# First expert's rows in four parts of a tile, the other experts' one-hot lanes behind them, strips that take token tiles in turn, and a GELU placed ahead of the search

## The chip, the cores and the metric

The kernel runs on one core of a Trainium2 chip. Its metric is the device time of one execution in microseconds (us), the median of several runs; lower is better. The profile is of one execution and has a time of its own.

## The reference

There are 4096 tokens of 256 features, in 8 blocks of 512. Two layers follow each other, each added to its input after a layer norm. The first is linear attention with 16 heads and an MLP (256 to 1024 to 256). The second, which the change is about, is a mixture of 8 experts in which every expert chooses its own 512 tokens:

```python
scores = jax.nn.softmax(xf @ gate_w.T, axis=-1)
vals, idx = jax.lax.top_k(scores.T, k)          # k = 4096 / 8 = 512 tokens of each expert
y = xf[flat_idx].reshape(k, n, d)               # then a layer norm of each row
h = jax.nn.gelu(jnp.einsum('knd,nfd->knf', y, fc1s) + b1s, approximate=True)
out = (jnp.einsum('knf,ndf->knd', h, fc2s) + b2s) * kept_w[..., None]
xf = xf.at[flat_idx].add(out.reshape(k * n, d))
```

All of it is in float32.

## The kernel before

**Stages.** The attention layer runs block by block, and the last block ends with the gate: logits, `lm` (L883), a difference and a product `ex` (L885, L888), an Exp on ScalarE (L892), and the scores (L898). Then a search finds each expert's threshold score: 30 bisection steps of one chain each (L1337 on VectorE, L1342 on TensorE, L1349 on VectorE), followed by prefix sums that give every chosen token a slot in its expert's list (L1365 to L1404). Then the experts are worked one after the other.

**From slots to rows.** For expert e, `mark` (L1423) builds the left operand `num` from the slots of 32 token tiles in three VectorE instructions, and `lanes` (L1433) builds a one-hot tile `hot` of 128 x 128 lanes x 32 token tiles, in two halves h of 16 token tiles each. `sums_of` (L1442) multiplies them on TensorE: 32 bf16 matmuls into one PSUM tile `pi`, 8 rounds of 4 matmuls, one for each strip of 32 rows. Strip k takes token tiles 8k to 8k+7, so each round needs both halves of `hot`. `sums_out` (L1454, ScalarE) copies `pi` out, `numbers` (L1458, one fp32 matmul, two records in the trace) folds it, and `numbers_out` (L1464, VectorE) gives the list `idx`. Four indirect DMAs on GpSimd (`gather`, L1527, issued at L1469) fetch 128 rows each into `y`.

**From rows to the first layer.** `normalised` (L1537, VectorE) scales each 128 rows, `turn` (L1549) transposes them on TensorE, `turned` (L1558, ScalarE) applies the norm's weights and makes `yT`. `hidden` (L1568) is the first expert layer: for each f of 8 groups of hidden units, `phe` sums over two halves of the features (four records of the trace, since an fp32 matmul is two), and `hidden_out` (L1577) evicts it with a GELU into `hTe`. For expert 0 the 512 rows are worked in two halves of 256 columns (`HALVES`, L1517); for the other experts in one piece of 512. `weighted` (L1586) is the second layer, `pwe`, in four row groups j. `weighted_out` (L1595, ScalarE) and `with_bias` (L1602, VectorE) finish the rows `o`, which GpSimd adds into two tables in memory (`scatter`, L1479). From expert 3 on, each expert's chosen rows are also read back from the sum table (`zg`), finished and written to the output; the other rows go by blocks (`load_z` to `store`).

**What sets the order.** Everything from L1407 on is a list of tasks for a planner (L187). A task names its engine, an assumed duration, a due time, what it comes after, and a buffer it takes; the planner goes through an assumed timeline and emits the tasks engine by engine, so each engine gets a fixed order. Four PSUM buffers (`mm`) are shared by `pi`, `pn`, `phe` and `pwe`, two (`tr`) by the transposes. Experts' index work is due 15 us earlier for each expert, so that of experts 1 to 5 stands early. What is outside the planner's lists, such as the search, is put in order by the framework at build time, engine by engine.

The order of GpSimd's gathers in this kernel is: three of expert 0, three of expert 1, the fourth of expert 0, the fourth of expert 1, then experts 2 and 3.

Of the kernel before, what the change touches and what calls it, by code (L numbers as in the profile page):

```python
# [9 lines left out]
F32 = mybir.dt.float32  # L10
# [15 lines left out]
def performer_moe_kernel(  # L26
# [18 lines left out]
    nc = tc.nc  # L45
    P = 128
# [1271 lines left out]
    def low_bits():  # L1318
        lb_i = rp.tile([P, W], I32, tag="kb", name="lb_i", bufs=2)
        nc.vector.tensor_scalar(lb_i, pTf.bitcast(I32), 0x7FFF, None, ALU.bitwise_and)  # L1320
        yield
        nc.vector.tensor_copy(kl, lb_i)
        yield
        nc.vector.tensor_scalar(khs, kh, 32768.0, None, ALU.mult)
        yield

    def largest(keys, tag, beside):
# [22 lines left out]
            u = un  # L1350
        return u

    uh = largest(kh, "h", low_bits())
    hs = small.tile([P, 1], F32, tag="hs", name="hs")
    nc.vector.tensor_scalar(hs, uh, -0.5, 32768.0, ALU.add, ALU.mult)
# [53 lines left out]
    def in_mm(name, shape, label):  # L1409
        return ps_mm.tile(shape, F32, tag=f"mm{slot[name]}", name=label, bufs=1)  # L1410
# [28 lines left out]
            lane[:, :, q], ALU.is_equal,  # L1439
        )  # L1440

    def sums_of(e):  # L1442

        pi = in_mm(("I", e), [P, P], f"pi_{e}")
        for i in range(NC // 4):
            for k in range(4):
                q = 8 * k + i
                nc.tensor.matmul(
                    pi[32 * k : 32 * k + 32, :], nums[e % 2][:, q, :], hots[e][:, :, q],
                    start=(i == 0), stop=(i == NC // 4 - 1),  # L1450
                )
        pis[e] = pi

    def sums_out(e):  # L1454
        pis["s", e] = ep.tile([P, P], F32, tag="pis", name=f"pis_{e}")
# [54 lines left out]


    ys, yTs, ggs, zgs, hTs, zs, lns, rows_o = {}, {}, {}, {}, {}, {}, {}, {}
    L0 = E - 5
    EARLY = 15.0
    AHEAD = 2.0
    SPAN = 31.0
    HALVES = (range(0, NJ // 2), range(NJ // 2, NJ))  # L1517

    def landed(name, engine, weight, place, work, after, landing, **kw):

# [124 lines left out]
        nc.vector.tensor_tensor(zj[:, 0:D], zj[:, 0:D], zj[:, D:], ALU.add)  # L1645

    kept = {}
    J = range(NJ)
    for e in range(E):
        z0 = e * SPAN  # L1650
        i0 = -EARLY * e
        def task(name, engine, weight, place, *more, z0=z0, **kw):
            add(name, engine, weight, z0 + place, *more, **kw)

        task(("M", e), "DVE", 0.8, i0 - 27, lambda e=e: mark(e), [("I", e - 2)])
        for h in range(2):
            task(
                ("L", e, h), "DVE", 1.18, i0 - 26 + h, lambda e=e, h=h: lanes(e, h),
                [("M", e)] + ([("L", e, 0)] if h else []), take=None if h else "z",
            )  # L1660
        task(("I", e), "PE", 0.8, i0 - 23, lambda e=e: sums_of(e), [("L", e, 1)], take="mm", dense=0.2)
        task(
            ("Ie", e), "ACT", 0.35, i0 - 22, lambda e=e: sums_out(e), [("I", e), ("IN", e - 2)],
            back=("I", e),
        )
        task(("IN", e), "PE", 0.3, i0 - 21, lambda e=e: numbers(e), [("Ie", e)], take="mm", dense=0)
        task(
# [3 lines left out]
        for j in J:  # L1671
            landed(
                ("G", e, j), "POOL", 1.4, -24 + 2 * j,
                lambda e=e, j=j: gather(e, j),
                [("IX", e), ("K", e - 2)]
                + [("T", e - 2, c, i) for c in range(KD) for i in range(2 if e == 2 else 1)]
                + ([("Gi", e, j - 1)] if j else []), 2.2,
            )
        halves = HALVES if e == 0 else (J,)
        for i, js in enumerate(halves):  # L1680
            task(
                ("Y", e, i), "DVE", 0.36 * len(js), -12, lambda e=e, js=js: normalised(e, js),
                [("G", e, j) for j in js],
            )
            for c in range(KD):
                task(
                    ("T", e, c, i), "PE", 0.11 * len(js), -5 + c,
                    lambda e=e, c=c, js=js, i=i: turn(e, c, js, i),
                    [("Y", e, i)], take="tr", dense=0.1,
                )  # L1690
                task(
                    ("Te", e, c, i), "ACT", 0.2 + 0.14 * len(js), -4 + c,
                    lambda e=e, c=c, js=js, i=i: turned(e, c, js, i),
                    [("T", e, c, i)] + [("H", e - 2, f, 0) for f in range(NF)]
                    + ([("H", 0, f, 1) for f in range(NF)] if e == 2 else []),
                    back=("T", e, c, i),
                )
        task(
# [6 lines left out]
                [("W", e - 2, j, 1) for j in J], 12.0,  # L1705
            )

        for i, js in enumerate(halves):
            cols = slice(js[0] * P, (js[-1] + 1) * P)
            part = 1.0 / len(halves)  # L1710
            for f in range(NF):
                task(
                    ("H", e, f, i), "PE", 1.76 * part, 1.75 * part * f + 7 * i,
                    lambda e=e, f=f, cols=cols, i=i: hidden(e, f, cols, i),
                    [("Te", e, c, i) for c in range(KD)] + ([("LW", e)] if e else []), take="mm",
                )
                task(
                    ("He", e, f, i), "ACT", 0.2 + 0.49 * part, 1.75 * part * f + 7 * i + 1,
                    lambda e=e, f=f, cols=cols, i=i: hidden_out(e, f, cols, i),
                    [("H", e, f, i)] + [("W", e - 2, j, 1) for j in J], back=("H", e, f, i),  # L1720
                )
        for j in J:
            for h in range(2):
                task(
                    ("W", e, j, h), "PE", 1.76, 15 + 3.6 * j + 1.8 * h,
                    lambda e=e, j=j, h=h: weighted(e, j, h),
                    [("He", e, f, i) for f in range(NF) for i in range(len(halves))]
                    + ([("W", e, j, 0)] if h else []),
                    take=None if h else "mm",
                )  # L1730
# [140 lines left out]
```

## Time and profile before

| what | value |
|---|---|
| median of 3 runs | 909.25 us (909.17, 909.25, 912.75) |
| the profiled execution's own time | 905.74 us |
| its span in the trace | 904.0 us |
| TensorE busy, share of the span | 804.4 us, 89% |
| VectorE, ScalarE, GpSimd busy | 67%, 40%, 32% |
| last block's gate to the search's start | 589.8 to 601.2 us |
| search and slots | 602.3 to 636.7 us |
| first expert's index work and gathers | 636.7 to 656.0 us |
| first expert's first layer (`phe`) | 652.14 to 668.3 us |
| second layer of expert 0 to that of expert 7 (`pwe` to `pwe`) | 669.08 to 890.2 us |

How to read it: times in the views are microseconds from the span's start. PE is TensorE, PEld its weight loads, DVE VectorE, ACT ScalarE, POOL GpSimd, SP the queue of plain DMAs. A row "x4" stands for four instructions that follow each other; its time is from the first start to the last end. PEclk is the share of TensorE's clock that was granted. Two views carry most of what follows: the chain that ended last, in order of time, and the timeline of all engines in a window.

### The profile page before, as it was taken

Reading aid. Unit: us, or ns where it says so; the run is one execution under the profiler, and the core shown is the slowest. Engines: PE = TensorE matmul, PEld = TensorE weight load, DVE = VectorE, ACT = ScalarE, POOL = GpSimd, SP = SyncE. Lnnn points to the kernel's source line nnn. Section 1 sums busy time; section 2 is a strip of 40 time slices with the busy share of each in tenths; the row PEclk is TensorE's granted clock in tenths of the full one; section 3 lists DMA queues with packets and bytes.
Section 4 is the critical chain, followed back from the end, with each engine's and each line's share of the span. In section 5 each row is a group of like instructions: output and inputs, shape, how many; then the busy total and the mean of one; then the engine's idle time right before and its main releaser. Section 6 shows DMA issues by size and latency. Waiting matters only on the chain.

```text
span 904.0 us, 14999 instructions
## 1 busy us (share of the span) xinstructions
PE 804.4 (89%) x5792; PEld 561.8 (62%) x5792; DVE 604.7 (67%) x1590; ACT 359.4 (40%) x662; POOL 287.0 (32%) x395
## 2 busy tenths in 40 slices
PE   5987999999899999899999989941699999999993
PEld 2665585685585685486586578721485765677663
DVE  5488658889857889867798866867922211987233
ACT  2372624644734553643463562310243223222330
POOL 5210002112102112102102101430454666785784
PEclk9988999999999999999999999955799999999997
DMA  7000001302200400300300300174135558998641
GB/s 247 1 2 1 1 2 41 100 3 70 72 1 1 140 3 33 108 2 1 125 18 2 117 3 1 58 237 172 37 112 91 143 106 240 306 275 250 193 99 41
DMA packets 61687, 78.15 MB, mean 86 GB/s; under 512 B 7984, under 2 KB 52016, under 8 KB 61488
## 3 DMA queue, kind: packets, MB, share of 16 engines
q1 hardware_dynamic: 51056, 58.87, 20.1%
q0 software_dynamic: 9856, 17.46, 8.8%
q8 instruction: 45, 0.74, 0.4%
q10 hardware_dynamic: 704, 0.87, 0.3%
q14 instruction: 26, 0.21, 0.1%
HBM read 44.01 MB, written 33.18 MB: 85 GB/s over the span
## 4 chain that ended last, share of the span: by engine, by line
PE 63%; DVE 25%; POOL 5%; issue 5%; ACT 1%; DMA 0%; POOLq 0%; DVEq 0%; ACTq 0%
PE pwe L1590 11%; PE phe L1572 10%; PE pm L862 9%; PE ph L816 7%; PE ptq L698 3%; PE pv L564 3%; PE pc L609 3%; DVE r L169 2%; DVE mxk L522 2%; PE pxk L503 2%; PE pq L440 2%; DVE kp L525 2%; PE pw L797 2%; DVE sh L672 2%; PE pdiv L729 1%
## 5 line engine op out<-in xcount | busy, mean ns | idle before, releaser
L816 PE MATMUL ph<-xaT,w_sb 128*128 128x512 f32 (+1 forms) x288 | 118.7, 552 | 0.5 <-DVE r L873 0.5
L1572 PE MATMUL phe<-yT,w1e 128*128 128x512 f32 (+1 forms) x288 | 112.5, 547 | 0.2 <-ACT yT L1562 0.2
L1590 PE MATMUL pwe<-w2e,hTe 128*128 128x256 f32 x512 | 112.4, 379 | 0.0
L862 PE MATMUL pm<-w_sb,hT 128*128 128x256 f32 x448 | 105.8, 382 | 0.0
L1590 PEld LDWEIGHTS pwe<-w2e,hTe 128*128 128x128 f32 x512 | 96.6, 190 | 14.0 <-issue 1.3
L862 PEld LDWEIGHTS pm<-w_sb,hT 128*128 128x128 f32 x448 | 81.8, 190 | 11.9 <-issue 1.8
L1572 PEld LDWEIGHTS phe<-yT,w1e 128*128 128x128 f32 x288 | 54.1, 190 | 51.9 <-issue 49.6
L816 PEld LDWEIGHTS ph<-xaT,w_sb 128*128 128x128 f32 x288 | 53.3, 192 | 44.5 <-issue 36.7
L821 ACT ACTIVATE hT<-ph,cols_sb 128x512 f32<-128x512 f32 (+1 forms) x72 | 46.0, 640 | 68.1 <-PE ph L816 62.5
L1581 ACT ACTIVATE hTe<-phe,cols_sb 128x512 f32<-128x512 f32 (+1 forms) x72 | 46.0, 640 | 66.0 <-PE phe L1572 65.9
L589 ACT ACTIVATE kp<-kp,nstab 128x256 f32<-128x256 f32 x128 | 54.5, 496 | 10.6 <-DVE nstab L553 10.6
L1469 POOL DMA_INDIRECT y<-xg,idx x32 | 37.4, 1168 | 64.0 <-DVE num L1426 41.7
L1605 DVE SCALAR_TENSOR_TENSOR o<-b2s_sb,gg,o 128x256 f32<-128x256 f32 x32 | 15.4, 483 | 60.2 <-ACT o L1598 57.5
L1483 POOL DMA_INDIRECT accs<-o,idx x28 | 47.4, 1694 | 10.7 <-issue 5.4
L522 DVE TENSOR_REDUCE mxk<-pxk 128x8 f32<-128x512 f32 x64 | 43.6, 681 | 10.4 <-PE pxk L503 10.4
L1598 ACT ACTIVATE o<-pwe,gg 128x256 f32<-128x256 f32 x32 | 15.2, 474 | 88.3 <-PE pwe L1590 88.3
L157 POOL TENSOR_SCALAR rs_b<-mv_b 128x4 f32<-128x4 f32 (+1 forms) x9 | 2.4, 262 | 145.8 <-DVE mv_b L154 145.8
L709 ACT ACTIVATE qpT<-ptq 128x512 f32<-128x512 f32 x64 | 36.2, 595 | 29.2 <-PE ptq L698 28.9
L679 DVE TENSOR_TENSOR qd<-pxq,sh 128x512 f32<-128x512 f32 x64 | 42.8, 687 | 4.5 <-PE ptq L698 2.3
L698 PE MATMUL ptq<-ident,qd 128*128 128x128 f32 x256 | 37.2, 280 | 8.6 <-DVE ex L885 8.1
L525 DVE TENSOR_TENSOR kp<-pxk,diag 128x512 f32<-128x512 f32 x64 | 43.5, 680 | 0.0
L672 DVE TENSOR_REDUCE sh<-pxq 128x8 f32<-128x512 f32 x64 | 40.8, 678 | 2.6 <-PE pxq L503 2.6
(239 smaller groups left out, 1530.3 us busy)
## 6 DMA issues: line engine op xcount, KB each, us to landing
w1e<-in_f SPq DMA_DIRECT2D x8, 1024.0 KB, 7.0
w2e<-in_f SPq DMA_DIRECT2D x8, 1024.0 KB, 8.2
z<-acc SPq DMA_DIRECT2D x8, 1024.0 KB, 8.1
x<-in_x_in SPq DMA_DIRECT2D x8, 512.0 KB, 5.8
accs<-x SPq DMA_DIRECT2D x8, 512.0 KB, 3.1
acc<-x SPq DMA_DIRECT2D x8, 512.0 KB, 4.5
xg<-xf SPq DMA_DIRECT2D x8, 512.0 KB, 3.8
accs<-xf SPq DMA_DIRECT2D x8, 512.0 KB, 4.5
```

Source lines behind the costliest of these rows:

```text
L522: nc.vector.tensor_reduce(head_cols(note("mxk", b, [P, NT, H])[:, t, :], c), pxs, AX.X, ALU.max)
L525: nc.vector.tensor_tensor(heads(get("kp", b)[:, t, :, :], c), pxs, head_cols(diag(b, 0, t), c) .unsqueeze(3).to_broadcast([P, 4, 2, M]), A ...
L589: nc.scalar.activation(kp[:, :, h, :], kp[:, :, h, :], AF.Exp, bias=nstab[:, h : h + 1])
L672: nc.vector.tensor_reduce(head_cols(kept["sh", b, t], i), pxs[:, :, i, :, :], AX.X, ALU.max,)
L698: nc.tensor.transpose(pt[:, i, :], get("qd", u)[:, 2 * hp : 2 * hp + 2, :].rearrange("p h m -> p (h m)"), ident,)
L816: nc.tensor.matmul(ph, w1_sb[:, c, ts(f, P)], get("xaT", b)[:, c, cols], start=(c == 0), stop=(c == KD - 1),)
L821: nc.scalar.activation(get("hT", b)[:, f, cols], ph, AF.Relu, bias=cols_sb[:, C_B1 + f : C_B1 + f + 1])
L862: nc.tensor.matmul(kept["PM", b, t, 0], get("hT", b)[:, f, ts(t, P)], w2_sb[:, f, :], start=(f == 0), stop=(f == NF - 1),)
L1483: this = nc.gpsimd.indirect_dma_start(out=table[:, :], out_offset=bass.IndirectOffsetOnAxis(ap=idxs[e][:, j : j + 1], axis=0), in_=src, in ...
L1572: nc.tensor.matmul(ph, w1e[:, c, ts(f, P)], yT[:, c, cols], start=(c == 0), stop=(c == KD - 1))
L1581: nc.scalar.activation(hTs[e][:, f, cols], kept["H", e, f, i], AF.Gelu_apprx_tanh, bias=cols_sb[:, col : col + 1],)
L1590: nc.tensor.matmul(kept["W", e, j], hTs[e][:, f, ts(j, P)], ws[e][1][:, f, :], start=(f == 0), stop=(f == NF - 1),)
```

## The change

Four edits go together.

1. After the search's helpers a new tile `idle` is written by a GELU on ScalarE from `one_c` (a column of ones), ahead of the call of the search in the text of the program.
2. A strip takes token tiles in turn: q is 4i + k and not 8k + i. For expert 0 `sums_of` is two tasks, rounds 0 to 3 (token tiles 0 to 15, the first half of `hot`) and rounds 4 to 7. For the other experts it stays one task.
3. The marks of experts 1 to 7, and so their lanes, come after the last part of expert 0's rows is normalised.
4. Expert 0's rows are worked in four parts of 128 columns and not in two of 256: normalising, transposes, `yT`, `phe` and its GELU. Due times follow from the number of parts.

```diff
+    idle = rp.tile([P, 1], F32, name="idle")
+    nc.scalar.activation(idle, one_c, AF.Gelu_apprx_tanh)
     uh = largest(kh, "h", low_bits())
...
-    def sums_of(e):
-        pi = in_mm(("I", e), [P, P], f"pi_{e}")
-        for i in range(NC // 4):
+    def sums_of(e, rounds=range(NC // 4)):
+        if rounds[0] == 0:
+            pis[e] = in_mm(("I", e) if len(rounds) == NC // 4 else ("Ia", e), [P, P], f"pi_{e}")
+        pi = pis[e]
+        for i in rounds:
             for k in range(4):
-                q = 8 * k + i
+                q = 4 * i + k
...
-    HALVES = (range(0, NJ // 2), range(NJ // 2, NJ))
+    PARTS = [range(j, j + 1) for j in J]
+    NPARTS = len(PARTS)
...
-        task(("M", e), "DVE", 0.8, i0 - 27, lambda e=e: mark(e), [("I", e - 2)])
+        task(
+            ("M", e), "DVE", 0.8, i0 - 27, lambda e=e: mark(e),
+            [("I", e - 2)] + ([("Y", 0, NPARTS - 1)] if e else []),
+        )
...
-        task(("I", e), "PE", 0.8, i0 - 23, lambda e=e: sums_of(e), [("L", e, 1)], take="mm", dense=0.2)
+        if e == 0:
+            task(
+                ("Ia", e), "PE", 0.7, -24, lambda e=e: sums_of(e, range(NC // 8)), [("L", e, 0)],
+                take="mm", dense=0.1,
+            )
+            task(
+                ("I", e), "PE", 0.7, -23, lambda e=e: sums_of(e, range(NC // 8, NC // 4)),
+                [("L", e, 1), ("Ia", e)], dense=0.1,
+            )
+        else:
+            task(
+                ("I", e), "PE", 1.2, i0 - 23, lambda e=e: sums_of(e), [("L", e, 1)], take="mm",
+                dense=0.2,
+            )
...
-        halves = HALVES if e == 0 else (J,)
-        for i, js in enumerate(halves):
+        parts = PARTS if e == 0 else (J,)
+        for i, js in enumerate(parts):
...
-            part = 1.0 / len(halves)
+            part = 1.0 / len(parts)
             for f in range(NF):
                 task(
-                    ("H", e, f, i), "PE", 1.76 * part, 1.75 * part * f + 7 * i,
+                    ("H", e, f, i), "PE", 1.76 * part, 1.75 * part * f + 14 * part * i,
```

The remaining lines of the diff carry the four parts into what waits for expert 0's first layer and transposes.

Since the planner replays its list, the order of every engine changes from here on. In the order of the changed program GpSimd gathers all four parts of expert 0, then all of expert 1, then of expert 2; those of expert 3 stand between the scatters of expert 0. On TensorE the transposes of the four parts stand between the first `phe` of part 0; the `pi` blocks of experts 1, 2 and 3 stand after `phe` f = 3 of part 1, after f = 4 of part 2, and after the last `phe` of part 3; the transposes of expert 1 stand within the last row group of expert 0's `pwe`. ScalarE's order around the new GELU is:

```
L944  TensorCopy plT<-pl
L1355 LoadActFuncSet
L1355 Activation idle<-one_c
L892  LoadActFuncSet
L892  Activation ex<-ex
L1460 TensorCopy pis<-pi
L1568 Activation yT<-pt_y (two)
L1587 LoadActFuncSet
L1587 Activation hTe<-phe
```

In the kernel before, `ex` follows `plT` with nothing between, and the one LoadActFuncSet of this stretch is the one ahead of the first `hTe`.

More of the change, by code (lines that the diff above doesn't have):

```diff
@@ L1451, in sums_of @@
                 )
-        pis[e] = pi
     def sums_out(e):
@@ L1512, in performer_moe_kernel @@
     ys, yTs, ggs, zgs, hTs, zs, lns, rows_o = {}, {}, {}, {}, {}, {}, {}, {}
+    J = range(NJ)
     L0 = E - 5
@@ L1647, in performer_moe_kernel @@
     kept = {}
-    J = range(NJ)
     for e in range(E):
@@ L1660, in performer_moe_kernel @@
             )
-        task(("I", e), "PE", 0.8, i0 - 23, lambda e=e: sums_of(e), [("L", e, 1)], take="mm", dense=0.2)
+        if e == 0:
[12 more added lines that the diff above has]
+            )
         task(
             ("Ie", e), "ACT", 0.35, i0 - 22, lambda e=e: sums_out(e), [("I", e), ("IN", e - 2)],
-            back=("I", e),
+            back=("I", e) if e else ("Ia", e),
         )
@@ L1675, in performer_moe_kernel @@
                 [("IX", e), ("K", e - 2)]
-                + [("T", e - 2, c, i) for c in range(KD) for i in range(2 if e == 2 else 1)]
+                + [("T", e - 2, c, i) for c in range(KD) for i in range(NPARTS if e == 2 else 1)]
                 + ([("Gi", e, j - 1)] if j else []), 2.2,
             )
-        halves = HALVES if e == 0 else (J,)
-        for i, js in enumerate(halves):
+        parts = PARTS if e == 0 else (J,)
+        for i, js in enumerate(parts):
             task(
@@ L1694, in performer_moe_kernel @@
                     [("T", e, c, i)] + [("H", e - 2, f, 0) for f in range(NF)]
-                    + ([("H", 0, f, 1) for f in range(NF)] if e == 2 else []),
+                    + ([("H", 0, f, i) for f in range(NF) for i in range(1, NPARTS)] if e == 2 else []),
                     back=("T", e, c, i),
@@ L1706, in performer_moe_kernel @@
             )
-        for i, js in enumerate(halves):
+        for i, js in enumerate(parts):
             cols = slice(js[0] * P, (js[-1] + 1) * P)
-            part = 1.0 / len(halves)
+            part = 1.0 / len(parts)
             for f in range(NF):
                 task(
-                    ("H", e, f, i), "PE", 1.76 * part, 1.75 * part * f + 7 * i,
+                    ("H", e, f, i), "PE", 1.76 * part, 1.75 * part * f + 14 * part * i,
                     lambda e=e, f=f, cols=cols, i=i: hidden(e, f, cols, i),
@@ L1717, in performer_moe_kernel @@
                 task(
-                    ("He", e, f, i), "ACT", 0.2 + 0.49 * part, 1.75 * part * f + 7 * i + 1,
+                    ("He", e, f, i), "ACT", 0.2 + 0.49 * part, 1.75 * part * f + 14 * part * i + 1,
                     lambda e=e, f=f, cols=cols, i=i: hidden_out(e, f, cols, i),
@@ L1726, in performer_moe_kernel @@
                     lambda e=e, j=j, h=h: weighted(e, j, h),
-                    [("He", e, f, i) for f in range(NF) for i in range(len(halves))]
+                    [("He", e, f, i) for f in range(NF) for i in range(len(parts))]
                     + ([("W", e, j, 0)] if h else []),
```

## The prediction

> **What bounds the kernel now.** I read the busy table by slices first, then the chain that ended last in order of time, then the timeline around the places where the chain leaves TensorE. The slices:
>
> ```profile
> PE   5987999999899999899999989941699999999993
> PEclk9988999999999999999999999955799999999997
> ```
>
> Each figure is a fortieth of the span, 22.6 us. TensorE is full except in three slices around 600 to 640 us, and there its granted clock is at half. The windows view says the same of what follows: from 669.1 to 890.2 us TensorE is busy 221.01 of 221.10 us. So whatever comes late before 669 is late at the end. The changed stretch lies there; the chain through it:
>
> ```profile
> 637.55 2.36 DVE hot L1437 x2
> ...
> 649.22 1.09 POOL y L1469
> ...
> 654.44 3.45 DMA y<-xg,idx
> 657.91 0.37 DVE y L1541
> 658.32 0.55 PE pt_y L1555 x3
> 658.87 9.50 PE phe L1572 x44
> ```
>
> The fourth gather of expert 0 is issued only at 654.44, behind three of expert 1, and TensorE waits for it until 658.32. The timeline has the rest:
>
> ```profile
> 638.83 0.38 PE L1448 MATMUL pi<-hot,num 128*32 128x128 bf16 x2 [3.96 <-DVE hot L1437]
> 639.97 1.90 PE L1448 MATMUL pi<-hot,num 128*32 128x128 bf16 x30 [0.75 <-DVE hot L1437]
> 642.90 0.16 DVE L1466 CAST idx<-pn 128x4 int32<-128x4 f32 x1
> 643.37 1.40 POOL L1469 DMA_INDIRECT y<-xg,idx  x1 [41.67 <-DVE num L1426]
> 645.07 1.89 POOL L1469 DMA_INDIRECT y<-xg,idx  x1 [0.30 <-issue]
> 652.14 4.61 PE L1572 MATMUL phe<-yT,w1e 128*128 128x256 f32 x20 [0.22 <-ACT yT L1562]
> 652.56 1.28 ACT L1581 ACT_TABLE_LOAD   x1
> ```
>
> Two matmuls of `pi` start at 638.83, and 30 must wait for the second half of `hot`. The gathers take 1.40 to 1.91 us while lanes are built on DVE, and 1.01 later. Between 641.9 and 651.1 TensorE is not idle: it does the `pi` blocks of experts 1 to 3. That decides this case.
>
> **Edit 1, the GELU.** In the built order it does not stand in the search but ahead of the last Exp, and the Exp gets a table load of its own. Here is the place:
>
> ```profile
> 598.97 0.27 ACT L944 COPY plT<-pl 128x128 f32<-128x128 f32 x1 [1.20 <-PE pl L937]
> 600.54 0.23 ACT L892 ACTIVATE ex<-ex 128x32 f32<-128x32 f32 x1 [1.31 <-DVE ex L888]
> ```
>
> ScalarE is free from 599.24. A load takes 1.28 (row 652.56), a small ACTIVATE about 0.2 (`ex` takes 0.23), a second load 1.28: with the gaps of 0.02 the Exp starts at 602.05 and not 600.54, 1.5 later. Scores, search and everything after hang on it, so **+1.5**. Bounds: 0, if the first load is hidden in some way I don't see, and 1.5; the gap of 1.31 already covers one of the loads. The load before the first `hTe` stays, since Exp has replaced the table; it is covered, because `phe` has three more PSUM buffers to run into.
>
> The row shows a GELU at 653.86, 0.02 after its load. The Trainium skill, "ScalarE: Activation LUTs", section "What ACT_TABLE_LOAD costs", adds a drain of about 1.38 to each 1.283, 2.66 per switch; by that the Exp would come 4.2 late and the sum below would be 2.7 higher. The trace shows no such drain, so I go by the row.
>
> **Edit 2, the strips.** A round of four matmuls takes 0.216 (30 in 1.90, the last lasting 0.39: 7 further rounds in 1.51). Now four rounds run beside the second half of `hot` and four after 639.97: `pi` ends 4 x 0.216 = 0.86 earlier, at 641.01. `idx` ends at 642.20 and not 643.06, as DVE is no longer building lanes; the first gather starts 0.31 later, at 642.51.
>
> **Edit 3, the lanes behind.** DVE is quiet during the four gathers, so I take 1.01 each and 0.30 between (rows from 660.65). Rows of expert 2 land 1.86 after a gather's end (1.80 to 1.92, by the starts of L1541). The four parts land at 645.4, 646.7, 648.0 and 649.3, where the last now comes at 657.9. If the first gather keeps its 1.40, all is 0.4 later. The wait put on the marks holds up DVE alone: behind it stand the marks and lanes of expert 1, done about 649.7 + 0.8 + 2.4 = 652.9; TensorE wants them about 655.
>
> From 645.4: normalise 0.35, transpose 0.44 at half clock (row 596.70), `yT` of 128 columns about 0.45 (256 take 0.56, 512 take 0.775): `phe` starts at **646.75 and not 652.14**, 5.4 earlier.
>
> **Edit 4, four parts, and what TensorE must now do.** A fp32 record with 128 columns has its price in this row:
>
> ```profile
> 69.67 0.97 PEld L774 LDWEIGHTS pr<-rden,spread 128*128 128x128 f32 x8 [0.17 <-issue]
> ```
>
> (0.97 - 0.19)/7 = 0.111, against 0.216 for 256 columns (4.61 less the last's 0.38, over 19, with one start-up gap). Part work is 8 x 4 x 4 = 128 records, 14.25 us, where 64 took 13.8: +0.45. From 646.75 to the first `pwe` TensorE has those 14.25, six transposes 0.65, three `pi` blocks 3 x 8 x 0.216 = 5.2, two `pn` 0.5: 20.6, so 667.35. The transposes of expert 1 (0.88) and a `pn` (0.25), which before lie ahead of `pwe`, lie behind: compared like with like 668.5 against 669.08, **-0.6**. The 5.4 and the stall of 1.5 go to the 5.2 of `pi`, which lost their cover.
>
> **The clock.** TensorE is now idle from 642.0 to 645.8. The windows view has the clock at 0.50 until 642.0 and 0.66 on average over 642.0 to 645.6, so it rose near 644.45, 5.6 after `pi` began. With the dense work now beginning at 645.8 I put the rise at 651.4. Until then a record takes twice as long (four `pl` of 128 columns in 1.06 at 597.82, the last 0.42: 0.214 each). Half of 4.65 us, less little waiting, is **+2.2**. Bounds: 0, if the clock is up at 646.75, and 4.2, if it takes as long as the row that is worst here (589.9 to 600.0: TensorE busy 7.49 of 10.10 at clock 0.50), a rise at 655.8. I take the 5.6, the same matmuls in the same place.
>
> "TensorE: Matmul & The Clock Gate", Part 1, speaks against this edit too: full clock comes after a busy window of some 3.4 us, whose start is not tied to the kernel. As an estimate by that page the rise is 3.4 to 6.8 after 645.8, and the sum +1.4 to +3.0.
>
> **The end.** The tail's order changes. Now:
>
> ```profile
> 890.15 0.47 ACT L1598 ACTIVATE o<-pwe,gg 128x256 f32<-128x256 f32 x1 [2.98 <-PE pwe L1590]
> 892.17 0.48 DVE L1605 SCALAR_TENSOR_TENSOR o<-b2s_sb,gg,o 128x256 f32<-128x256 f32 x1
> ```
>
> The last `o` waits 1.55 on DVE behind the row before it, because GpSimd came to the first row's root only at 883.52. In the new order that `o` stands before the finish of row 2 (0.41 + 0.43), which comes between it and its sum: 1.55 - 0.84 = 0.7 gained, **-0.65**. Against that, GpSimd has one more output scatter (1.3) behind the last scatter-add of expert 6; if it is late there, the end is +0.65 to +1.3 instead. The rest of the dense stage has the same instructions; its new order hides under TensorE.
>
> **Sum.** +1.5 - 0.6 + 2.2 - 0.65 = **+2.45 us**. The profiled execution took 905.74 (span 904.0 and 1.7 around it), so 908.2 there. The runs' median is 3.5 above it, so I forecast 909.25 + 2.45 = **911.7**. A difference of 0.5% (4.5 us) is about what can be told from none; this is less.
>
> **Rivals.**
> 1. *Slower by over 0.5%: the half clock lasts.* ScalarE's chain in the first part (eight `yT` between GELUs, and a load of 1.28) makes TensorE wait between records, so the clock stays down while it works. Each us past 651.4 costs about 0.45. It decides from (4.5 - 2.45)/0.45 = 4.6 us on, a rise after 656.0; at 658 the time is 914.7. For: 589.9 to 600.0. Against: at half clock a `phe` takes 0.85 on TensorE and under 0.4 on ScalarE, so TensorE is dense. 0.14.
> 2. *The edits do what they are said to do:* the first load serves, the Exp does not move, the clock is up by 648.5 (+0.8). Sum 0 - 0.6 + 0.8 - 0.65 = -0.45: 908.8. Against: the second load in the built order. 0.12.
> 3. *GpSimd late in the tail:* +1.5 - 0.6 + 2.2 + 1.3 = +4.4, at the bound: 913.6. 0.10.
> 4. *Faster by over 0.5%:* the waits removed (5.4 and 1.5) count whole and `pi` goes into gaps of TensorE: -6.9 + 1.5 = -5.4, 903.9. Against: 221.01 of 221.10 has no gaps. 0.03.
>
> The forecast has 0.61. Rivals 2 and 3 are within 0.5%, save a quarter of 3 put with slower: same 0.805, slower 0.165, faster 0.03. **Range:** the bounds beside 911.7 are clock -2.2 and +2.0, table -1.5, tail +1.95, gathers +0.4, and the runs before spread by 3.6. Not all fall on one side: 907.2 to 916.5.
>
> **What would show it.** Two table loads between `plT` and the last `ex`, and `ex` 1.5 later. Against that moved clock: `pi` of expert 0 done 0.86 earlier, gathers of 1.01, the fourth part landing some 8 us earlier, `phe` starting 5.4 earlier, three `pi` blocks between records of `phe`, and a first `pwe` within 1 us of 669.5 + 1.5. PEclk at half when `phe` starts. The forecast is wrong if the clock is full at `phe`'s start or half past 656, or if a gather without lanes beside it still takes 1.9.

## The result, and the profile after

| | before | after |
|---|---|---|
| median of 6 runs each | 909.55 us (908.84 to 912.75) | 918.93 us (916.29 to 922.87) |
| ratio | | 1.010, 95% interval 1.007 to 1.013 |
| the profiled execution, its span | 905.74, 904.0 | 919.93, 918.2 |

The change makes the kernel about 9.4 us slower. I had forecast +2.45 and a range up to 916.5, so the result lies outside. The two profiled executions differ by 14.2, and the first thing to find out is how much of that belongs to the change. I cut both traces at the same five places:

| stretch, by instructions that both kernels have | before | after | more |
|---|---|---|---|
| start to `plT` of the last block (code that the change does not touch) | 598.97 | 602.57 | 3.60 |
| `plT` to the last `ex` | 1.58 | 3.09 | 1.51 |
| `ex` to the first `hot` (the search) | 37.01 | 37.02 | 0.01 |
| first `hot` to the first `phe` of expert 1 (**the head**) | 45.34 | 49.08 | 3.74 |
| from there to the last `o` on ScalarE (the dense stage) | 207.26 | 207.70 | 0.44 |
| last `o` to the end of the span (**the tail**) | 13.89 | 18.76 | 4.87 |

The first row is not the change. The windows view, whose columns behind the window are its length, the busy times of PE, PEld, DVE, ACT and POOL with their counts, the granted clock, the DMA share and GB/s, shows where it comes from; first before, then after:

```profile
50.00:100.00 50.00, 41.96 (x424) 29.43 (x425) 42.93 (x90) 25.27 (x49) 6.14 (x5) 0.86 0.00 1
...
500.00:550.00 50.00, 47.13 (x462) 34.13 (x461) 36.31 (x88) 26.78 (x52) 4.80 (x10) 1.00 0.16 51
```

```profile
50.00:100.00 50.00, 38.24 (x416) 27.71 (x417) 40.27 (x80) 22.11 (x43) 5.90 (x4) 0.83 0.00 1
...
500.00:550.00 50.00, 47.12 (x433) 33.83 (x435) 35.08 (x86) 27.08 (x53) 4.79 (x10) 0.97 0.17 54
```

The same code had 0.86 and 1.00 of the clock in one execution, 0.83 and 0.97 in the other: 6 hundredths of 50 us, so 3.0 us of clock, most of the 3.60. In the sixteen profiles of this case that `plT` starts anywhere from 598.4 to 607.4. What the change did is the other 10.6 us: 1.5, 3.7, 0.4 and 4.9. That is near the 9.4 of the medians.

**The table.** ScalarE's timeline of the kernel after:

```profile
602.57 0.27 ACT L944 COPY plT<-pl 128x128 f32<-128x128 f32 x1 [1.21 <-PE pl L937]
602.85 1.28 ACT L1355 ACT_TABLE_LOAD   x1
604.14 0.20 ACT L1355 ACTIVATE idle<-one_c 128x1 f32<-128x1 f32 x1
604.37 1.28 ACT L892 ACT_TABLE_LOAD   x1
605.66 0.23 ACT L892 ACTIVATE ex<-ex 128x32 f32<-128x32 f32 x1
```

Two loads, and `ex` 3.09 behind `plT`: the order and the price are those of the forecast. GELU and Exp each start 0.01 after their load has ended.

**The head.** The timeline around the gathers:

```profile
643.96 2.25 PE L1453 MATMUL pi<-hot,num 128*32 128x128 bf16 x32 [3.96 <-DVE hot L1440]
...
647.25 0.16 DVE L1470 CAST idx<-pn 128x4 int32<-128x4 f32 x1 [2.21 <-PE pn L1465]
647.73 1.38 POOL L1473 DMA_INDIRECT y<-xg,idx  x1 [40.91 <-DVE idx L1470]
649.41 1.01 POOL L1473 DMA_INDIRECT y<-xg,idx  x1 [0.30 <-issue]
...
651.38 0.66 PE L1561 MATMUL pt_y<-ident,y 128*128 128x128 f32 x2 [4.16 <-DVE y L1547]
...
652.37 1.01 PE L1578 MATMUL phe<-yT,w1e 128*128 128x128 f32 x3 [0.34 <-ACT yT L1568]
```

`phe` now starts 9.69 us after the first `hot` and not 14.59. But TensorE, which did the `pi` blocks of experts 1 to 3 in that wait, is idle for 4.16 us ahead of the transposes, and the windows show what that does to its clock (the last number but two):

```profile
644.00:648.00 4.00, 2.78 (x34) 1.41 (x33) 1.20 (x2) 0.27 (x1) 0.27 (x1) 0.56 0.02 4
648.00:652.00 4.00, 0.62 (x2) 0.29 (x2) 0.35 (x1) 0.14 (x1) 3.13 (x3) 0.87 0.25 68
652.00:656.00 4.00, 3.66 (x18) 3.63 (x18) 1.76 (x7) 3.51 (x8) 1.01 (x1) 0.50 0.26 68
656.00:660.00 4.00, 4.00 (x30) 4.00 (x30) 3.93 (x7) 3.10 (x11) 0.00 (x0) 0.78 0.00 0
```

0.56 of 644 to 648 is half a clock until 647.5, then full; 0.87 is full until 650.9; 0.78 is half until 657.8. The clock came up for `pi`, fell again in the wait, and 5.4 us of `phe` ran at half. In the kernel before, the `pi` blocks filled the wait and the clock stayed up:

```profile
648.00:652.00 4.00, 3.42 (x42) 1.96 (x40) 3.62 (x10) 1.01 (x4) 3.39 (x3) 1.00 0.31 84
```

And in the chain that ended last the `pi` blocks stand between records of `phe`, with nothing beside them:

```profile
661.22 1.97 PE pi L1453 x25
663.19 1.09 PE phe L1578 x8
664.28 0.12 PE pn L1465 x2
664.40 3.23 PE phe L1578 x28
667.63 1.96 PE pi L1453 x26
...
674.91 1.90 PE pi L1453 x30
676.82 12.29 PE pwe L1596 x56
```

**The tail.** GpSimd's timeline, from the gathers of expert 7's sums on (L1473), past the root of expert 6's rows and its first output scatter (L1487), to the root of expert 7's first row. The last `o` is at 899.47:

```profile
885.62 1.08 POOL L1473 DMA_INDIRECT zg<-accs,idx  x1 [0.30 <-issue]
...
890.71 0.25 POOL L157 TENSOR_SCALAR rs_r<-mv_r 128x4 f32<-128x4 f32 x1
...
895.06 1.11 POOL L1487 DMA_INDIRECT out<-zg,idx  x1 [2.91 <-DVE zg L1636]
...
900.12 0.26 POOL L157 TENSOR_SCALAR rs_r<-mv_r 128x1 f32<-128x1 f32 x1
```

The root of expert 7's first row comes 0.65 after the last `o`; in the kernel before it came 6.6 ahead of it, with the last `o` at 890.15:

```profile
883.52 0.26 POOL L157 TENSOR_SCALAR rs_r<-mv_r 128x1 f32<-128x1 f32 x1
```

GpSimd was behind, and the four rows had to be finished after TensorE had ended.

### The profile page after: what moved, and what is told of

Same layout as the page of the kernel before. It is cut to its first block, busy times and chain, and to the rows that moved or that the text cites. A ratio compares the mean times of both kernels' runs of the same rounds, so it can differ in the third digit from the quotient of the medians.

```text
span 918.2 us, 15143 instructions
## 1 busy us (share of the span) xinstructions
PE 808.5 (88%) x5856; PEld 567.2 (62%) x5856; DVE 605.2 (66%) x1590; ACT 367.1 (40%) x685; POOL 279.9 (30%) x395
## 3 DMA queue, kind: packets, MB, share of 16 engines
q1 hardware_dynamic: 51056, 58.87, 19.5%
## 4 chain that ended last, share of the span: by engine, by line
PE 66%; DVE 18%; issue 8%; POOL 5%; ACT 1%; DMA 1%; POOLq 0%; DVEq 0%; ACTq 0%
PE phe L1578 11%; PE pwe L1596 11%; PE pm L862 10%; PE ph L816 7%; PE pc L609 3%; PE ptq L698 3%; PE pv L564 3%; DVE r L169 2%; DVE mxk L522 2%; PE pxk L503 2%; PE pq L440 2%; DVE kp L525 2%; PE pw L797 2%; PE pi L1453 1%; PE pdiv L729 1%
## 5 line engine op out<-in xcount | busy, mean ns | idle before, releaser
L1578 PE MATMUL phe<-yT,w1e 128*128 128x512 f32 (+1 forms) x352 | 116.5, 488 | 0.3 <-ACT yT L1568 0.3
L1578 PEld LDWEIGHTS phe<-yT,w1e 128*128 128x128 f32 x352 | 59.3, 199 | 51.6 <-issue 50.6
L1587 ACT ACTIVATE hTe<-phe,cols_sb 128x512 f32<-128x512 f32 (+1 forms) x88 | 50.0, 572 | 64.1 <-PE phe L1578 62.6
L1473 POOL DMA_INDIRECT y<-xg,idx x32 | 33.8, 1056 | 71.7 <-DVE idx L1470 40.9
L1487 POOL DMA_INDIRECT accs<-o,idx x28 | 45.9, 1638 | 17.1 <-issue 4.4
L609 PE MATMUL pc<-kp,v_aug 128*34 128x128 f32 x512 | 34.1, 285 | 8.4 <-DVE kp L595 8.4
```

The costliest lines, as they stand in the source:

```text
L609: nc.tensor.matmul(pc[s * 64 : s * 64 + 2 * (DH + 1), i, :], v_aug[:, t, pair, :].rearrange("p h d -> p (h d)"), kp[:, t, pair, :].rearran ...
L1487: this = nc.gpsimd.indirect_dma_start(out=table[:, :], out_offset=bass.IndirectOffsetOnAxis(ap=idxs[e][:, j : j + 1], axis=0), in_=src, in ...
L1578: nc.tensor.matmul(ph, w1e[:, c, ts(f, P)], yT[:, c, cols], start=(c == 0), stop=(c == KD - 1))
L1587: nc.scalar.activation(hTs[e][:, f, cols], kept["H", e, f, i], AF.Gelu_apprx_tanh, bias=cols_sb[:, col : col + 1],)
```

## The experiments

My theory after this (A in the texts below): three causes add up. Two table loads, 1.5; a head in which TensorE loses the work that covered its wait, and its clock with it, 3.7; a tail in which a new order makes GpSimd late, 4.9. Rivals stand with each run. Since executions of one kernel differ by some us, I read the stretches of the table above in each profile first, and the medians second. A median "of before" is that of the runs on the same chip.

### x1: the tail's order held

```diff
+    PINNED = {
+        'POOL': [('Qi', 3, 0), ('Qi', 3, 1), ...],
+        'DVE': [('S', 0), ('WB', 3, 0), ...],
+    }
+    for names in PINNED.values():
+        for one, two in zip(names, names[1:]):
+            t = tasks[two]
+            tasks[two] = t[:4] + (list(t[4]) + [one],) + t[5:]
     give_out()
```

The lists, cut here at `...`, hold the order of the kernel before from expert 3's sums on.

> The changed kernel, with the order of GpSimd's and VectorE's tasks from expert 3's sums on held to that of the kernel before (the planner is given that order as a chain; nothing else differs, TensorE's and ScalarE's orders are those of the changed kernel). Theory A, three causes: two table loads ahead of the Exp (+1.5), a head in which TensorE idles, loses its clock and then does the pi blocks without cover (+3.7), and a tail in which GpSimd's new order is late (+4.9). By it the stretch from the last o on ScalarE to the span's end goes from 18.8 us back to 13.9 +- 0.7, TensorE's stages before it stay as they are, and the time is 918.9 - 4.9 = 914.0. Rival B, GpSimd has too much to do in the tail whatever its order, or its tail is late because it is fed late: the stretch stays at 18 to 19 us and the time at 918.9. Rival C, the whole difference is clock windows that fell badly: neither changes by more than 1.

Measured: tail 14.0, median 915.8 against 911.3 before, ratio 1.0067 (1.0041 to 1.0092); the median is 1.8 above theory A's 914.0, its range 913.8 to 918.7. The same four places of GpSimd, with the last `o` at 899.19:

```profile
879.53 0.26 POOL L157 TENSOR_SCALAR rs_r<-mv_r 128x4 f32<-128x4 f32 x1
...
881.11 1.29 POOL L1473 DMA_INDIRECT zg<-accs,idx  x1 [0.20 <-issue]
...
887.60 1.03 POOL L1487 DMA_INDIRECT out<-zg,idx  x1 [0.21 <-issue]
...
892.55 0.26 POOL L157 TENSOR_SCALAR rs_r<-mv_r 128x1 f32<-128x1 f32 x1
```

With TensorE's end within 0.3 us of where it was, the tail is back. Rivals B and C fall: the 4.9 are the order of GpSimd and VectorE. The later runs agree: the nine profiles with that order held have tails of 12.5 to 15.3, the five without it (the kernel after, x2, x3, x11, x13) 18.4 to 19.5. The two engines were held together, so which of them matters more is not shown. Nor is it shown which edit moved their order, except that it was not the GELU: x2, which leaves it out, has a tail of 19.1.

### x2 and x3: no GELU, and the GELU where the change's words put it

```diff
-    idle = rp.tile([P, 1], F32, name="idle")
-    nc.scalar.activation(idle, one_c, AF.Gelu_apprx_tanh)
```

> The changed kernel without edit 1, the GELU (the tile idle is left out). Theory A: plT to the last ex is 1.57 again and not 3.1, everything after it comes 1.5 earlier: 917.4. Rival, each switch of table costs a drain of 1.38 besides its load: 2.7 to 4.2 earlier, 914.7 to 916.2. Rival, the loads were hidden in a wait of VectorE or of the gate: 0, 918.9.

```diff
-    nc.scalar.activation(idle, one_c, AF.Gelu_apprx_tanh)
+    nc.scalar.activation(idle, kh[:, 0:1], AF.Gelu_apprx_tanh)
```

> The changed kernel with the GELU reading one column of kh, which is computed from the scores, and no longer the column of ones: so it must come behind the last Exp, and its table load stands in the search, as the change's words say. Theory A: the Exp is 1.5 earlier, as without the GELU, there is no load ahead of the first hTe, and that is worth nothing more, since phe had PSUM buffers to run into: 917.4, the first pwe within 0.3 us of where it is without the GELU, counted from the first hot. Rival, the load of 1.28 ahead of the first hTe held up TensorE: another 1.3 earlier, 916.1.

Measured: `plT` to `ex` 1.58 in both, the 1.5 of theory A. From the first `hot` to expert 1's first `phe` 48.36 without the GELU and 48.34 with it in the search. ScalarE's timeline of x3:

```profile
606.03 0.23 ACT L892 ACTIVATE ex<-ex 128x32 f32<-128x32 f32 x1 [1.31 <-DVE ex L888]
606.27 1.28 ACT L1355 ACT_TABLE_LOAD   x1
```

The load stands in the search and there is none ahead of the first `hTe`, and nothing gets faster by it: it had been covered all along. The medians, 917.2 and 919.2, are too far spread (912.4 to 924.2) to show 1.5.

### x4: the clock held

x1 and 64 more bf16 matmuls (each of the 32 token tiles twice), into a buffer that nobody reads, in TensorE's idle stretch.

```diff
+    def beside():
+        pd = in_mm(("D", 0), [P, P], "pd")
+        for i in range(NC // 2):
+            for k in range(4):
+                nc.tensor.matmul(
+                    pd[32 * k : 32 * k + 32, :], nums[0][:, 2 * i + k // 2, :],
+                    hots[0][:, :, 2 * i + k // 2], start=(i == 0), stop=(i == NC // 2 - 1),
+                )
...
+            task(("D", e), "PE", 3.6, -20.5, beside, [("IN", e)], take="mm")
```

> The kernel of the held tail order with 64 more bf16 matmuls on TensorE (the first two token tiles' worth of pi's operands, taken many times into a spare PSUM buffer that nobody reads) between pn of expert 0 and the first transpose, where TensorE was idle for some 4 us; nothing of the output depends on them. Theory A, the clock fell to half in this idle stretch and stayed there for two of its steps of 3.41 us: now it is full from about 2 us after pi until the dense stage ends, the first 30 records of phe take 0.112 and not 0.22 us, and the first pwe comes 2.7 us earlier: 914.0 - 2.7 = 911.3. Rival, the clock falls for the narrow records themselves or for waits between them: half steps still lie within phe, and the time is 914.0 or, if the added matmuls delay the transposes, up to 1 more.

Measured: 46.99 from hot to expert 1's first `phe`, against 47.65 in x1 and 49.08 in the kernel after; median 914.2, ratio 1.0029 (1.0010 to 1.0048). The windows of x4:

```profile
648.00:652.00 4.00, 4.00 (x66) 2.10 (x65) 0.19 (x2) 0.00 (x0) 2.61 (x3) 0.96 0.11 34
652.00:656.00 4.00, 3.23 (x25) 2.50 (x21) 1.07 (x4) 3.21 (x7) 1.81 (x2) 1.00 0.40 102
656.00:660.00 4.00, 4.00 (x34) 3.88 (x35) 3.86 (x10) 3.90 (x14) 0.00 (x0) 1.00 0.02 4
```

More work on TensorE makes the head shorter, by 0.7 against x1, and no half clock is left within `phe` (the clock is granted in steps of 3.41 us, see the end): it was the idle stretch that took the clock or kept it down. The medians of x4 and x1 differ by 1.7, with intervals that overlap. The size missed: the 2.7 came from the profile of the kernel after, but x1's own had the half clock only until 655.7, 2.4 us into `phe`, and loses 0.7 by it where the kernel after loses 2.1. How much is lost differs from run to run. In all eight profiles with the lanes behind and nothing put in the wait, `phe` starts at half clock and stays there for 2.4 to 5.7 us. In the five with all three `pi` blocks in the wait (before, x7, x10, x12, x14) no half clock reaches `phe`; in the two with two of the three (x5, x8) it has 3.2 and 3.4 us of it.

### x5, x6 and x9: lanes behind or free, parts wide or narrow

x5 is x1 without edit 3, x9 is x1 without edit 4; x6 is the kernel before with edit 3 alone, its tail order held.

```diff
 x5
-            [("I", e - 2)] + ([("Y", 0, NPARTS - 1)] if e else []),
+            [("I", e - 2)],
 x6
-        task(("M", e), "DVE", 0.8, i0 - 27, lambda e=e: mark(e), [("I", e - 2)])
+        task(("M", e), "DVE", 0.8, i0 - 27, lambda e=e: mark(e), [("I", e - 2)] + ([("Y", 0, 1)] if e else []))
 x9
-    PARTS = [range(j, j + 1) for j in J]
+    PARTS = [range(0, NJ // 2), range(NJ // 2, NJ)]
```

> The changed kernel with the held tail order and without edit 3: the marks of experts 1 to 7 don't wait for expert 0's rows, so the pi blocks of experts 1 to 3 stand ahead of the first transposes again, as in the kernel before. Four narrow parts and the strips in turn stay. Measured so far from the first hot to expert 1's first phe: before 45.3 us, held tail order 47.7, the same with the clock held 47.0. Theory A (edit 3 takes from TensorE the work that covered the wait for the rows, and the clock with it): no half clock within phe, the gathers take up to 1.9 again, phe starts 13 to 15 us after hot and not 9.6, and yet the stretch to expert 1's first phe is 44.5 to 45.5; time 915.8 - 2.5 = 913.3. Rival, the narrow records and the many small transposes cost the time: the stretch stays at 47 or more, and the time at 915.8.

> The kernel before with edit 3 alone: the marks of experts 1 to 7 come behind the second half of expert 0's rows (tail order held to that of before). Wide parts, strips as before, no GELU. Theory A: phe starts about 12.1 us after the first hot and not 14.6, then come 13.8 of phe, 5.6 of three pi blocks, 0.5 of pn and 0.4 of transposes, so that expert 1's first phe is at 47.3 from hot, and 1 to 2 later where the clock falls in the idle stretch: 48 +- 1 against 45.3, and the time 911.3 + 2.7 = 914. Rival, edit 3 is a gain by itself (gathers of 1.0 instead of 1.9, no stall in phe) and the narrow parts lose it: 45.3 or less, 911 or less.

> The changed kernel with the held tail order and without edit 4: expert 0's rows in two halves of 256 columns, lanes still behind them, strips in turn, GELU as in the change. It closes a square of two edits (lanes free or behind, wide or narrow parts). Measured from the first hot to expert 1's first phe: lanes free and wide 45.3 (before; 42.8 with the gathers first), free and narrow 46.2, behind and narrow 47.7 to 49.1 (as the clock's steps fall). Theory A: edit 3 costs 4 us whatever the parts, since three pi blocks, the clock and the wait for the rows lose their cover; wide parts start 1.3 later and save 1 to 2 in records: 49.0 +- 1, time 916. Rival, the narrow parts are what costs: below 47, time 913 or less.

Measured, and set beside the others. All times in us; the middle columns are TensorE's time between the first `phe` of expert 0 and that of expert 1, each record counted to the next one's start or to its own end:

| kernel | `phe` starts, from hot | `phe` | `pi`, `pn` | `pt_y` | `pwe` | idle | expert 1's `phe`, from hot |
|---|---|---|---|---|---|---|---|
| before | 14.59 | 13.94 | 0 | 1.53 | 13.82 | 1.46 | 45.34 |
| after | 9.69 | 17.19 | 6.26 | 1.95 | 14.00 | 0 | 49.08 |
| x4, clock held | 9.54 | 15.38 | 6.13 | 1.91 | 14.00 | 0.02 | 46.99 |
| x5, lanes free | 12.23 | 15.85 | 2.13 | 1.58 | 14.00 | 0.35 | 46.15 |
| x6, edit 3 alone | 11.91 | 16.32 | 5.93 | 1.67 | 14.00 | 0 | 49.83 |
| x9, wide, behind | 11.10 | 16.84 | 6.19 | 1.73 | 14.00 | 0 | 49.87 |
| x7, strips and rows first | 13.75 | 13.94 | 0 | 1.31 | 13.82 | 0 | 42.82 |
| x10, x7 with narrow records | 13.73 | 14.63 | 0 | 1.31 | 13.82 | 0 | 43.48 |

Medians: x5 912.7, ratio 1.0018 (0.9998 to 1.0038); x6 913.9, 1.0035 (1.0012 to 1.0058); x9 916.4, 1.0072 (1.0044 to 1.0100). Edit 3 alone starts `phe` 2.7 earlier and ends 4.5 later: 5.9 of `pi` and `pn` without cover, and 2.4 more in `phe` at half clock. That is theory A's mechanism, 0.8 above its range because the half clock reached 4.3 us into `phe`. With the lanes behind, wide parts are no better than narrow ones (x9, 49.87), so the rivals of x6 and x9, that the narrow parts cost the time, fall. x5 came out at 46.15, between theory A's 45.5 and the rival's 47: one `pi` block stayed without cover (it is due after `phe` in the planner's new order), and 3.2 us of half clock fell into its `phe` (0.59 of the clock in 656 to 660), which theory A had not expected; `phe` started at 12.2, ahead of its 13 to 15.

### x7, x8, x12 and x14: what is good in the change

x7 is the kernel before with edit 2 and the due time below, its tail order held. x8 is the kernel after without edits 1 and 3, with that due time and the tail order held. x12 is edit 2 alone, also with the tail order held, x14 the due time alone.

```diff
-                ("G", e, j), "POOL", 1.4, -24 + 2 * j,
+                ("G", e, j), "POOL", 1.4, -24 + 2 * j - (16 if e == 0 else 0),
```

> The kernel before with edit 2 alone and one due time: the gathers of expert 0 are due 16 us earlier in the planner, so all four go ahead of expert 1's (tail order held). The lanes of the other experts stay beside the gathers and their pi blocks in the wait for the rows. Theory A: pi of expert 0 ends 0.8 us earlier, the fourth part of the rows lands some 4 us earlier and the stall of 1.5 within phe is gone, the clock stays up: expert 1's first phe 43.0 +- 0.7 us from hot against 45.3, time 911.3 - 2.3 = 909.0. Rival, the stall only moves (the second half waits for VectorE, which is building lanes): 44.5, 910.4.

> The changed kernel without edits 1 and 3, with expert 0's gathers due first and the tail order held: what stays of the change are the strips in turn and the four narrow parts. Theory A: as the kernel before with the strips in turn and the gathers first, but phe can start one gather earlier and costs 0.6 to 1.2 more for its narrow records: expert 1's first phe 43.3 +- 1 us from hot, time 909.3. Rival, narrow parts lose the time by their records and by a chain of eight yT on ScalarE, where the clock falls: 45 or more, 911 or more.

> The kernel before with edit 2 alone (strips in turn, expert 0's pi as two tasks; tail order held). Theory A: pi ends 0.8 earlier, but idx does not: on VectorE it stands behind the second half of expert 1's lanes, as before (5.3 us after the first hot in both kernels that leave the lanes there). So the edit is worth nothing alone, 45.3 +- 0.3 from hot to expert 1's first phe, and 910.9; what the kernel with the gathers first gained, it gained by the gathers. Rival, the 0.8 goes through: 44.5, 910.1.

> The kernel before with one number changed: expert 0's gathers are due 16 us earlier, so the fourth goes ahead of expert 1's. Nothing else; GpSimd's tail order is unchanged. Theory A: the wait for the fourth part of the rows (1.5 us of TensorE in the middle of phe) goes and nothing comes in its place: 43.3 +- 0.4 us from the first hot to expert 1's first phe, against 45.3 before, 44.8 with the strips alone and 42.8 with both; time 910.5 - 2.0 = 908.5. Rival, without the strips the rows come as late as before, since VectorE builds lanes ahead of them: 44.8 or more, 910.

Measured, from hot to expert 1's first `phe`: x7 42.82, x8 45.87, x12 44.83, x14 43.65. Medians and ratios: x7 908.7, 0.9972 (0.9952 to 0.9992); x8 911.1, 1.0014 (0.9995 to 1.0033); x12 910.1, 0.9994 (0.9973 to 1.0014); x14 909.5, 0.9990 (0.9969 to 1.0012). The chain of x7 has no wait left between `hot` and `pwe`:

```profile
655.35 1.10 PE pi L1450 x15
656.45 0.39 PE pt_y L1556 x2
...
656.86 0.57 ACT yT L1563
...
657.48 2.02 PE phe L1573 x8
659.50 0.44 PE pt_y L1556 x4
659.94 12.09 PE phe L1573 x56
```

x7 is 0.3% faster than the kernel before, and so faster than both. Of the four it is the only one whose interval lies clear of 1: the head of x14 is shorter by 1.7, but its median cannot be told from the kernel before. x7's 2.5 us of head are 1.7 of the rows fetched first (x14: the stall of 1.46 is gone, and 0.22 in transposes) and about 0.8 of the strips. In x12 I was wrong: `idx` is indeed hardly earlier (5.30 after hot, 5.35 before), but each `pi` block ends 0.8 sooner after its lanes, and the first transposes, which stand behind the last of them, start 12.65 after hot and not 13.50. Of that 0.8, 0.3 goes into a longer stall (1.79), since the fourth part of the rows comes no earlier. In x8 theory A's 43.3 is wrong and the rival right: `phe` starts 1.6 earlier than in x7, but costs 1.7 more (15.63) in narrow records and a step of half clock, and a `pi` block of 1.9 is left over for the time after it.

### x10: the narrow records by themselves

```diff
-        for c in range(KD):
-            nc.tensor.matmul(
-                ph, w1e[:, c, ts(f, P)], yT[:, c, cols], start=(c == 0), stop=(c == KD - 1)
-            )
+        n = cols.stop - cols.start
+        for a in range(0, n, P if e == 0 else n):
+            w = P if e == 0 else n
+            for c in range(KD):
+                nc.tensor.matmul(
+                    ph[:, a : a + w], w1e[:, c, ts(f, P)],
+                    yT[:, c, cols.start + a : cols.start + a + w],
+                    start=(c == 0), stop=(c == KD - 1),
+                )
```

> The kernel that has the strips in turn and expert 0's gathers first (42.8 us from hot to expert 1's first phe, 908.7), with one thing changed: each phe of expert 0 sums its 256 columns in two pieces of 128, so 128 records instead of 64; order, transposes, GELUs and waits are as they were. The narrow records by themselves: theory A, 0.115 to 0.127 each (16.2 us for 128 with the clock held, against 14.3 for 64 wide ones): +1 to +1.9, so 43.8 to 44.7 and 910.1 +- 0.5. Rival, as I priced them in the prediction, 0.111 each: +0.45, 43.3.

Measured: +0.66 from hot to expert 1's first `phe`, median 907.5, ratio 0.9967 (0.9941 to 0.9993). The groups by form, x7 and then x10 (busy time, mean ns):

```profile
L1573 PE MATMUL phe<-yT,w1e 128*128 128x256 f32 x64 | 14.3, 381 | 0.2 <-ACT yT L1563 0.2
```

```profile
L1576 PE MATMUL phe<-yT,w1e 128*128 128x128 f32 x128 | 15.0, 277 | 0.2 <-ACT yT L1563 0.2
```

Between my two values: 14.63 / 128 = 0.114 a record and not 0.111, and a wide one 0.218. x10's median is not above x7's, though 1.4 more was expected. Its tail was 13.97 where x7's was 14.86, and tails of the held order differ by more than 0.66 for a reason that stays open (last section); whether the 0.66 reaches the end of the kernel is not shown.

### x11 and x13: where GpSimd's delay is made

x11 is the kernel after with one edge; x13 is the kernel after, its order held as in x1 but only from expert 5's sums on.

```diff
                 ("Q", e, j), "POOL", 1.4, -2 + 1.5 * j, lambda e=e, j=j: gather_sum(e, j),
-                [("A1", e - 1, i) for i in J], 3.2,
+                [("A1", e - 1, i) for i in J] + ([("RR", 6)] if e == 7 else []), 3.2,
```

> The changed kernel with one edge more in the planner: the gathers of expert 7's sums come behind the root of expert 6's rows, as in the kernel before; GpSimd's and VectorE's order up to there is that of the changed kernel, TensorE's and ScalarE's all along. In the changed kernel those gathers go first, and expert 6's four output scatters come 7 us later against the last o. Theory A: GpSimd's delay is from the experts before (its scatter-adds run 14 us behind their rows in expert 4, where they ran 6 behind before) and this one place is worth little: the stretch from the last o to the end goes from 18.8 to 17.5 to 18.8, time 918. Rival, the place near the end is what costs: 16 or less, time 916.

> The changed kernel with GpSimd's and VectorE's order held to that of before only from the gathers of expert 5's sums on (on VectorE from expert 5's first biased o); experts 3 and 4 and the block work beside them stay in the changed kernel's order. The other half of the split needs no run: held over experts 3 and 4 only, the planner arrives by itself at the very order of the kernel with the tail held (stretch from the last o to the end 14.0). Theory A: the delay is made at experts 3 and 4 (scatter-adds 14 us behind their rows) and GpSimd, which has no slack later, hands it on: the stretch is 17 or more (the changed kernel has 18.8) and the time 917 or more. Rival, the delay is made by the order from expert 5 on: 14 to 15, and 914 to 915.

Measured: tails 19.5 and 18.4, medians 921.1 and 919.8; theory A in both (x11 even above its 18.8). To hold the order near the end gives back nothing in x11 and 0.4 in x13. How far the scatter-adds of an expert's four rows start behind the `o` of ScalarE, from the traces:

| expert | before | after | x1 |
|---|---|---|---|
| 3 | 3.3, 3.1, 2.9, 4.7 | 2.8, 3.9, **8.5, 7.4** | 2.2, 2.1, 2.1, 2.1 |
| 4 | 7.5, 6.0, 6.5, 5.1 | 13.9, 12.4, 13.5, 14.3 | 6.1, 4.6, 4.7, 3.3 |
| 6 | 5.2, 3.8, 4.0, 3.7 | 11.3, 9.7, 8.2, 7.9 | 5.2, 3.8, 4.0, 3.7 |

It begins at expert 3's third row. There the planner's timeline, 1.9 us later in its own count (at the first read of expert 3's sums) while the due times are fixed, finds VectorE and GpSimd free for the block work first. GpSimd's timeline after; the roots `rs_z` are those of blocks of finished tokens:

```profile
785.64 1.04 POOL L158 TENSOR_TENSOR rs_z<-rs_z,mhalf 128x4 f32<-128x4 f32 x1
787.57 0.30 POOL L157 TENSOR_SCALAR rs_z<-mv_z 128x4 f32<-128x4 f32 x1 [0.89 <-DVE mv_z L154]
787.95 1.05 POOL L158 TENSOR_TENSOR rs_z<-rs_z,mhalf 128x4 f32<-128x4 f32 x1
791.67 1.68 POOL L1487 DMA_INDIRECT accs<-o,idx  x1 [2.62 <-DVE o L1611]
794.09 1.62 POOL L1487 DMA_INDIRECT accs<-o,idx  x1 [0.70 <-DVE o L1611]
...
803.65 1.47 POOL L1473 DMA_INDIRECT zg<-accs,idx  x1 [5.72 <-DMA accs<-o,idx]
...
818.61 1.63 POOL L1487 DMA_INDIRECT accs<-o,idx  x1 [4.08 <-DVE y L1547]
```

A block's root goes ahead of two scatter-adds, whose rows wait on VectorE behind the block's sums; the next expert's sums can be read only when these have landed (803.65, in x1 796.48), and its scatter-adds start at 818.61, in x1 at 810.49. After that GpSimd does not catch up to the end: against the kernel before it is 6 to 9 us later at expert 4 and still 4 to 6 at expert 6.

## Why the prediction was wrong, point by point

- **Bound now**: right for TensorE: the dense stage passes on what is late ahead of it and adds 0.4. But 4.9 of the 10.6 show behind TensorE's last work, on engines that this paragraph left out.
- **Edit 1, +1.5**: right, 1.51, with the reason. The Trainium skill, "ScalarE: Activation LUTs", section "What ACT_TABLE_LOAD costs", gives a drain of about 1.38 on top of the load. No run here shows one: GELU and Exp follow their loads by 0.01.
- **Edit 2, `pi` 0.86 earlier**: 0.78 (3.53 from hot against 4.31).
- **Edit 3, `phe` 5.4 earlier**: 4.9. The first gather kept 1.38, the bound I had named (0.4).
- **Three `pi` blocks without cover, 5.2**: right as a mechanism; in size 5.83, or 1.90 to 1.97 a block, and 5.51 in x6, which keeps the strips as they were. **Narrow records, +0.45**: 0.66 by x10; the row that I took the price from is one of weight loads, not of matmuls.
- **The head, -0.6**: with the clock held it is +1.65 (46.99 against 45.34). The terms that were too small are, in us: `phe`'s start 0.3 (9.54 where I had 9.2), `pi` 0.5, the 128 records of `phe` 0.4 (14.63 in x10 where I had 14.25), transposes 0.4, `pwe` 0.2; `pn` was 0.3 too large (0.43 for three where I had 0.75). What is left, 0.75, lies in `phe` itself (15.38 in x4, 14.63 for the same 128 records in x10): in some ten single records that take 0.18 to 0.26 where the others take 0.11, several of them just ahead of a `pi` block or a transpose. Why they do stays open.
- **The clock, +2.2**: 2.1 in the profiled execution (x4 against after), 0.7 in x1's. The mechanism was right, the closeness of the size is partly luck: I had one rise, 4.65 into `phe`. In this execution there was a rise for `pi`, a fall in the idle stretch, and a second rise 5.4 into `phe`; in the seven other profiles with the lanes behind there was one rise, 2.4 to 5.7 into it. The Trainium skill, "TensorE: Matmul & The Clock Gate", Part 1, has full clock come after a busy window of some 3.4 us that is not tied to the kernel; the traces agree on the window, with steps of 3.41 us (below).
- **The tail, -0.65**: this step failed, by 5.5 us, and it is the step that made the forecast wrong. Against the forecast of +2.45 the two profiles differ by 10.6 from `plT` on: of the 8.1 between, 5.5 are the tail, 2.1 the head with its clock (3.7 where I had 1.6) and 0.4 the dense stage. The prediction said "The rest of the dense stage has the same instructions; its new order hides under TensorE". I counted its instructions, and looked at their order only at the end. They do hide under TensorE, but GpSimd and VectorE work against each other there with little slack, a delay that begins at expert 3 (5.6 us in its third row) is 7.3 at the root of expert 7's first row, and behind TensorE's end nothing hides it (x1: with the order held the tail is back at 14.0).
- **Rival 3**, GpSimd late in the tail, was the right mechanism at the wrong price and place: 1.3 for one output scatter, where it came to 4.9, made 100 us earlier (x11, x13). Rival 1 needed a rise past 656.0; taken back by the 5.1 us by which this execution's search ended later, the rise was at 652.6. Rivals 2 and 4 did not happen.
- **The range** held the bounds of each term near the change; for what follows it had only the +1.95 of the tail.

## What to carry to other kernels

Work that fills a wait is not free to move because it is "not needed yet": here three blocks of 1.9 us covered the wait and kept half clock out of `phe`, and moving them behind it cost more than the shorter wait gave (edit 3 alone +4.5 in the head). When a planner replays its list, compare the whole order of each engine and not only the changed place, and ask of each engine off the critical path how late it comes to the last row: that lag, followed expert by expert, showed in one table what the busy shares did not. And the piece of the change that was worth most in the head, the first rows fetched first, needed one due time; a gain of the whole kernel that is clear of the spread, 0.3%, was measured only together with the strips (x7, x10).

## What the runs showed of the hardware that I had not expected

- The granted clock changes in steps of 3.41 us: in every trace the stretches at half clock are 1 to 4, 12, 16, 18 or 19 whole steps long, save the last one, which the end cuts off. The steps' places do not follow the kernel. In untouched code one execution had 5 of them up to 580 us (before), another 7 (after); a step at half clock loses half its work, 1.7 us, so two more make most of the 3.6 us of the first table. Over the sixteen profiles the two go together: with 5 or 6 such steps `plT` starts at 598.4 to 599.0, with 7 at 602.2 to 603.6, with 8 to 10 at 602.8 to 607.4. That the runs of one kernel lie up to 12 us apart (x2) may have the same cause in part; that is argued, not shown.
- Mostly a step's clock followed TensorE's busy share of the step before. In the kernel after: full after a step that was 0.78 busy (to 647.5), half after one without a matmul (to 650.9), still half after one 0.77 busy, full after a full one (657.8). It is no sharp bound: x14 fell to half for one step after a share of 0.84. And in all sixteen traces the clock fell for one step near 33 us, after a step in which TensorE counts as busy throughout; in the kernel after that step, 29.65 to 33.06, is mostly filled by matmuls of one column (L1252). Why it fell there stays open.
- With strips in turn the stretch from expert 1's first `phe` to the last `o` is 207.5 to 207.8 in all thirteen kernels that have them, 207.26 in the three that don't (before, x6, x14). The four `pi` blocks in it take some 0.1 more each (1.90 to 1.98 where it was 1.84). Why was not tried.
- With the tail order held, the tail was still between 12.5 (x5) and 15.3 (x4). What sets that stays open.
